# Ten products with C instead of eight on GpSimd in each 24 tiles of a selective scan

## The chip, the core and the metric

The kernel runs on one core of one Trainium2 chip. A core has five engines that run side by side, each with its own queue of instructions: PE (TensorE, matrix products), DVE (VectorE), ACT (ScalarE), POOL (GpSimd) and SP (SyncE, which here issues the transfers). They meet at semaphores. The metric is the time of one execution on the device in microseconds (us); lower is better.

## What is computed

The input is x, 4 images of 96 channels by 64 x 64 pixels, in float32. Four layers follow one another, for each image by itself:

- Layer 0 is a state-space block: layer norm, a projection to 192 inner channels, a 3 x 3 depthwise convolution, and a selective scan over the 4096 pixels in four directions (rows, columns, and both backwards); then a norm, a gate, a projection and an MLP with GELU.
- Layer 1 is a smaller block of the same kind with one state per channel and two directions.
- Layer 2 mixes the tokens by a Fourier transform, followed by an MLP in 8-bit floats.
- Layer 3 is attention without softmax, and again an 8-bit MLP.

The scan of layer 0 is the largest part. For each image, direction, channel d (192) and state n (16) it computes, along the pixels t,

```
h[t] = h[t-1] * exp(dt[t] * A[d,n]) + dt[t] * x[t] * B[n,t]
y[t] = sum over n of h[t] * C[n,t]
```

## The kernel before

**Tiles.** The scan is cut into chunks of 1024 pixels: 4 batches x 4 directions x 4 chunks = 64 chunks. In one chunk there are 192 x 16 = 3072 sequences, which make 24 tiles of 128 partitions (32 channels by 4 states) by 1024 pixels; 1536 tiles in all. The function scan walks them in order. For each tile:

- L745, GpSimd: w = u * B, three tiles ahead (AHEAD). The tiles w lie in a ring of nine (W).
- L144 by way of decay (L731), ScalarE: h = exp(dt * A), two tiles ahead, into a ring of two.
- L821, VectorE: the scan itself, one instruction. It writes its result over w or over h.
- The product with C, in one of two places. If pool_out is true, the scan writes over w, and GpSimd multiplies w by C in place (L841) and copies the last state (L834). If not, the scan writes over h, VectorE multiplies (L829) and ScalarE copies the last state (L837). The copy is left out in the last chunk of a direction.
- L767, PE: the sums over the states, by a matmul with a 0/1 matrix, for pairs of tiles and three tiles later; L779 and L782, VectorE: the sums are added to y.

Which tiles go to GpSimd is decided by a number per batch:

```
POOL_OUT = (5, 8, 8, 8)
...
            pool_out = (x * POOL_OUT[b]) % 24 < POOL_OUT[b]
            o = w if pool_out else h
```

Here x is the tile's place in its chunk, 0 to 23. So 5 of 24 products are on GpSimd in batch 0, spread evenly, and 8 in the other batches.

**What runs beside the scan.** All other work of the program is written as generators, in one queue called stream: the fronts of the four batches (norm, convolution, preparation of dt, u, B and C), then for each batch, once its last direction has begun, its rest: tail (L856, the remainder of layer 0, four tasks of 1024 pixels), l1 (layer 1), transform, middle and back (layers 2 and 3; back ends with four tasks called second). A step of the stream issues some instructions on the engines. Between the instructions of one tile the kernel takes a step if its own account of times lets it:

```
    def advance(free, slack):
        late = max(chain["pe"] - 0.5, now["act"], now["pool"] - 6.0, now["pe"] - 2.0) - free
        if not put_off and late <= slack:
            step()
```

The account (now, chain, t_out and others) is kept while the program is built: each instruction adds its booked time to its engine, for instance 2.36 us for a product on GpSimd and 1.23 us for one on VectorE. So the order of all instructions on each engine is fixed when the program is built, and follows from the booked times. VectorE's part of the steps is put off (later) and issued between the scan's instructions (flush).

While the scan runs, a step works on one task at a time. MLP conversions and additions are given to GpSimd then (aside, L103). When the scan is over, the group in progress is finished (drained), the constants of layer 2 are loaded (L1567, 8 MB), and whatever is left of the stream runs with Now.width = 4: up to four tasks at a time, in tail two, and aside chooses VectorE.

Of the kernel before, what the change touches and what calls it, by code (L numbers as in the profile page):

```python
# [26 lines left out]

DIRS = (0, 1, 3, 2)

POOL_OUT = (5, 8, 8, 8)  # L30

AHEAD, W = 3, 9

# [23 lines left out]
def tile_hybrid(ctx: ExitStack, tc: tile.TileContext, I: dict, out: bass.AP):  # L57
# [597 lines left out]
    def scan(pls, advance, need, last_pass):  # L655
# [146 lines left out]
        for i, (ci, p, g, a) in enumerate(tiles):  # L802
# [12 lines left out]
            h, w = hs.pop(i), ws[i]  # L815
            pool_out = (x * POOL_OUT[b]) % 24 < POOL_OUT[b]
            o = w if pool_out else h
# [890 lines left out]
```

## Time and profile before

| what | us |
|---|---|
| median of 3 runs (6810.67 to 6836.49) | 6822.95 |
| the profiled execution | 6833.64 |
| its span, first to last instruction | 6831.9 |
| first scan starts | 97.2 |
| last scan starts | 6227.9 |
| from the end of the scan to the end of the span | about 600 |

The profile gives for each engine the time in which it was busy. Groups of instructions are shown as line, engine, operation, output<-inputs, shape and count, then the busy time and the mean duration in ns, then the idle time of the engine just before these instructions and the instruction that ended most of it. In the rows by stretch, the first number is the length, and then for each engine stand the busy time and, in brackets, the number of instructions; the granted clock is the share of full speed at which PE ran. A row of waits names the waiting instruction and the one that it waited for. Matmuls in float32 appear as two records each.

### The profile page before, as it was taken

Reading aid. Unit: us, or ns where it says so; the run is one execution under the profiler, and the core shown is the slowest. Engines: PE = TensorE matmul, PEld = TensorE weight load, DVE = VectorE, ACT = ScalarE, POOL = GpSimd, SP = SyncE. Lnnn points to the kernel's source line nnn. Section 1 sums busy time; section 2 is a strip of 40 time slices with the busy share of each in tenths; the row PEclk is TensorE's granted clock in tenths of the full one; section 3 lists DMA queues with packets and bytes.
Section 4 is the critical chain, followed back from the end, with each engine's and each line's share of the span. In section 5 each row is a group of like instructions: output and inputs, shape, how many; then the busy total and the mean of one; then the engine's idle time right before and its main releaser. Section 6 shows DMA issues by size and latency. Waiting matters only on the chain. (4 is left out here: it accounts for less than half of the span.)

```text
span 6831.9 us, 52664 instructions
## 1 busy us (share of the span) xinstructions
PE 4673.5 (68%) x15538; PEld 1514.0 (22%) x15538; DVE 5603.1 (82%) x3872; ACT 3731.0 (55%) x5242; POOL 5188.9 (76%) x2732
## 2 busy tenths in 40 slices
PE   6758667676677666666776675657676666576877
PEld 2112111121112124211111142211111332111353
DVE  3888779797789998998899998898999989984413
ACT  3556546666555545665555455566555456553337
POOL 4888879899779788998688898897887889972000
PEclk8768677686778778766777786668777876676987
DMA  5766666767544348444443375454434563442141
GB/s 149 217 194 193 185 180 192 208 207 210 156 132 143 116 136 262 137 146 144 134 151 125 98 262 155 131 158 139 143 128 127 189 209 127 133 144 83 43 125 37
DMA packets 502464, 1050.00 MB, mean 154 GB/s; under 512 B 138448, under 2 KB 252178, under 8 KB 501144
## 3 DMA queue, kind: packets, MB, share of 16 engines
q1 hardware_dynamic: 502176, 1046.63, 49.5%
q8 instruction: 123, 2.02, 0.1%
q14 instruction: 165, 1.35, 0.1%
HBM read 831.15 MB, written 211.09 MB: 153 GB/s over the span
## 5 line engine op out<-in xcount | busy, mean ns | idle before, releaser
L745 POOL TENSOR_TENSOR w<-u,bb 128x1024 f32<-128x1024 f32 x1536 | 3587.5, 2358 | 179.5 <-PE py L767 123.8
L144 ACT ACTIVATE h<-dt,negA 128x1024 f32<-128x1024 f32 x1536 | 1706.8, 1117 | 795.6 <-DVE w L829 429.2
L821 DVE TENSOR_TENSOR_SCAN h<-h,state,w 128x1024 f32<-128x1024 f32 x804 | 1886.8, 2347 | 271.9 <-ACT h L144 202.8
L829 DVE TENSOR_TENSOR w<-h,cc 128x1024 f32<-128x1024 f32 x1072 | 1309.0, 1221 | 56.7 <-DMA cc<-bc_d 18.8
L767 PE MATMUL py<-w,idup 128*32 128x512 f32 x6144 | 1125.3, 805 | 244.1 <-POOL w L841 80.9
L841 POOL TENSOR_TENSOR w<-w,cc 128x1024 f32<-128x1024 f32 x464 | 1092.0, 2353 | 188.3 <-DVE w L821 142.4
L821 DVE TENSOR_TENSOR_SCAN w<-h,state,w 128x1024 f32<-128x1024 f32 x348 | 814.5, 2341 | 50.9 <-ACT h L144 29.2
L837 ACT COPY state<-h 128x1 f32<-128x1 f32 x804 | 127.5, 159 | 1279.4 <-DVE w L829 1278.6
L821 DVE TENSOR_TENSOR_SCAN h<-h,w 128x1024 f32<-128x1024 f32 x268 | 612.9, 2287 | 103.6 <-ACT h L144 73.5
L98 PE MATMUL pc<-xp 97*64 97x512 f32 (+1 forms) x1152 | 400.2, 611 | 12.4 <-DMA xp<-wc_d 7.8
L767 PEld LDWEIGHTS py<-w,idup 128*32 128x32 f32 x6144 | 164.5, 126 | 1057.3 <-issue 597.3
L834 POOL COPY state<-w 128x1 f32<-128x1 f32 x348 | 64.3, 185 | 363.9 <-DVE w L821 363.1
L111 POOL TENSOR_TENSOR u<-dt,xi 128x512 f32<-128x512 f32 x160 | 216.8, 1371 | 156.7 <-ACT dt L144 142.3
L821 DVE TENSOR_TENSOR_SCAN w<-h,w 128x1024 f32<-128x1024 f32 x116 | 264.4, 2279 | 71.9 <-POOL w L745 55.1
L98 PE MATMUL pc<-xp,wc 96*96 96x512 f32 x576 | 275.1, 631 | 25.6 <-ACT u L144 25.6
L98 PE MATMUL pd<-xd,dtw 6*64 6x512 f32 (+1 forms) x512 | 211.4, 983 | 92.8 <-ACT xd L148 59.1
L98 PE MATMUL pcen<-t,cen 96*96 96x512 f32 x192 | 137.5, 853 | 161.3 <-POOL t L1332 78.8
L144 ACT ACT_TABLE_LOAD x176 | 225.8, 1283 | 32.0 <-PE pd L98 18.1
L136 ACT ACT_TABLE_LOAD x174 | 223.2, 1283 | 3.8 <-PEq L1698 0.7
L98 PEld LDWEIGHTS pc<-xp 97*64 97x64 f32 (+1 forms) x1152 | 149.9, 167 | 270.2 <-issue 239.4
L98 PE MATMUL po<-hq,q 128*96 128x512 fp8e5 x192 | 88.7, 586 | 163.0 <-POOL hq L1320 132.1
L98 PE MATMUL pvar<-sq,avg 96*96 96x512 f32 x256 | 168.9, 801 | 45.3 <-ACT sq L144 45.3
(242 smaller groups left out, 6330.8 us busy)
## 6 DMA issues: line engine op xcount, KB each, us to landing
u<-u_d SPq DMA_DIRECT2D x384, 512.0 KB
dt<-dt_d SPq DMA_DIRECT2D x384, 512.0 KB
bb<-bc_d SPq DMA_DIRECT2D x256, 512.0 KB
cc<-bc_d SPq DMA_DIRECT2D x256, 512.0 KB
dt_d<-dt SPq DMA_DIRECT2D x128, 256.0 KB
u_d<-u SPq DMA_DIRECT2D x128, 256.0 KB
f_d<-fo SPq DMA_DIRECT2D x64, 384.0 KB
a<-f_d SPq DMA_DIRECT2D x64, 384.0 KB
```

The source lines that it names most:

```text
L98: nc.tensor.matmul(o, lhsT=lhsT, rhs=rhs, **kw)
L111: aside(0.2 + size(o) * 2.1e-3, o, a, b).tensor_mul(o, a, b)
L136: nc.scalar.preload_act_table_set("natural_log_exp_and_others")
L144: nc.scalar.activation(o, i, func, **kw)
L745: pool.tensor_mul(w, us[ci, 2 * p + a], bbs[ci, g])
L767: nc.tensor.matmul(o, lhsT=idup, rhs=v, **flags)
L821: dve.tensor_tensor_scan(o[:, r], h[:, r], w[:, r], state if step else 0.0, ALU.mult, ALU.add)
L829: dve.tensor_mul(w, o, cc)
L834: pool.tensor_copy(state, o[:, last : last + 1])
L837: nc.scalar.copy(state, o[:, last : last + 1])
L841: pool.tensor_mul(w, o, cc)
```

## The change

From batch 1 on, 10 of 24 products with C are done by GpSimd instead of 8. Batch 0 keeps its 5.

```
-POOL_OUT = (5, 8, 8, 8)
+POOL_OUT = (5, 10, 10, 10)
```

The tiles that go to GpSimd are chosen by the same formula, so their places in a chunk change as well: with 8 it is each third tile, with 10 each second or third. For these tiles the scan writes over w instead of over h, GpSimd does the product and the copy of the state, and VectorE and ScalarE do neither. The booked times follow, and with them the places at which steps of the stream stand between the tiles.

## The prediction

> **What bounds the kernel now.** I read three views in this order: the page (which engines are loaded), the busy times by stretch (one row per batch of the scan, then what follows the scan), and the waits of VectorE and GpSimd inside the three batches that the change touches. From the page:
>
> ```profile
> PE 4673.5 (68%) x15538; PEld 1514.0 (22%) x15538; DVE 5603.1 (82%) x3872; ACT 3731.0 (55%) x5242; POOL 5188.9 (76%) x2732
> ...
> L745 POOL TENSOR_TENSOR w<-u,bb 128x1024 f32<-128x1024 f32 x1536 | 3587.5, 2358 | 179.5 <-PE py L767 123.8
> L821 DVE TENSOR_TENSOR_SCAN h<-h,state,w 128x1024 f32<-128x1024 f32 x804 | 1886.8, 2347 | 271.9 <-ACT h L144 202.8
> L829 DVE TENSOR_TENSOR w<-h,cc 128x1024 f32<-128x1024 f32 x1072 | 1309.0, 1221 | 56.7 <-DMA cc<-bc_d 18.8
> L841 POOL TENSOR_TENSOR w<-w,cc 128x1024 f32<-128x1024 f32 x464 | 1092.0, 2353 | 188.3 <-DVE w L821 142.4
> ```
>
> The product with C costs 1.22 us on VectorE and 2.35 us on GpSimd. Both engines are heavily loaded, so which one is late has to be read by stage. Busy time by stretch (columns: length, then PE, weight loads, VectorE, ScalarE, GpSimd, granted clock, DMA); the first four rows are batches 0 to 3 of the scan, the fifth is the tail of the last batch that was left over, the sixth the rest of the program:
>
> ```profile
> 97.00:1641.00 1544.00, 1105.32 (x3438) 297.23 (x3439) 1301.14 (x787) 895.51 (x1197) 1325.45 (x713) 0.73 0.66 198
> 1641.00:3158.00 1517.00, 996.67 (x3399) 316.51 (x3397) 1369.41 (x930) 839.07 (x1173) 1294.82 (x675) 0.73 0.49 155
> 3158.00:4707.00 1549.00, 1047.23 (x3487) 332.36 (x3488) 1383.24 (x954) 854.14 (x1201) 1284.77 (x664) 0.74 0.48 152
> 4707.00:6233.00 1526.00, 1024.58 (x3482) 328.82 (x3480) 1380.71 (x951) 852.62 (x1195) 1266.71 (x656) 0.74 0.45 143
> 6233.00:6320.00 87.00, 53.60 (x72) 14.24 (x72) 11.38 (x17) 20.05 (x30) 0.00 (x0) 0.59 0.33 122
> 6320.00:6832.00 512.00, 402.49 (x1544) 209.61 (x1544) 153.28 (x225) 245.64 (x413) 1.55 (x8) 0.83 0.26 68
> ```
>
> Batches 1 to 3 take 4592 us, in which VectorE is busy 4133 and GpSimd 3846: VectorE has the larger load and is idle 459 us. GpSimd is only 287 us below it. After the scan GpSimd does nothing, and the end is set by PE, ScalarE and transfers. Who is waited for in batches 1 to 3 (total us, times, longest):
>
> ```profile
> DVE h L821 <- ACT h L144: 207.4, 114, 13.5
> DVE y L779 <- PE py L767: 44.9, 21, 6.7
> DVE y L782 <- PE py L767: 44.4, 13, 10.3
> DVE h L821 <- POOL w L745: 29.5, 21, 3.0
> ...
> POOL state L834 <- DVE w L821: 343.9, 139, 11.9
> POOL w L841 <- DVE w L821: 132.8, 52, 8.6
> POOL w L745 <- PE py L767: 116.2, 52, 6.3
> ```
>
> VectorE waits for ScalarE's decay and PE's sums, hardly for GpSimd; GpSimd waits 477 us for the scans. Four single stretches show the extremes: one where VectorE binds, one where GpSimd binds, and the two clocks of the leftover tail.
>
> ```profile
> 2243.00:2553.00 310.00, 205.94 (x677) 61.92 (x680) 294.67 (x237) 153.76 (x210) 249.81 (x123) 0.74 0.39 123
> 2816.00:3158.00 342.00, 198.20 (x677) 55.60 (x676) 323.22 (x210) 220.86 (x323) 330.29 (x179) 0.70 0.42 136
> 6259.00:6304.00 45.00, 40.39 (x44) 9.39 (x45) 6.68 (x9) 10.13 (x16) 0.00 (x0) 0.50 0.07 18
> 6304.00:6320.00 16.00, 13.21 (x29) 4.85 (x27) 4.28 (x7) 9.91 (x14) 0.00 (x0) 0.96 0.00 0
> ```
>
> **The change: what moves.** Two tiles of each 24 change sides, in 48 chunks: 96 products. VectorE loses 96 x 1.221 = 117 us. GpSimd gains 96 x 2.353 = 226 us, and 72 state copies (the last chunk of a direction has none) at 0.185 = 13 us, together 239. ScalarE loses those 72 copies at 0.159 = 11 us; it is 55% busy, so I count nothing.
>
> The rest of a batch is placed by the planner, which books 2.36 us for every GpSimd product. In its account a chunk is 24 x 2.35 + 16 x 1.23 + 3 x 0.7 = 78.2 us of VectorE against 24 x 2.36 + 8 x 2.55 = 77.0 of GpSimd before, and 75.7 against 82.1 now. So by its books GpSimd is late, and it lets fewer steps of the rest run beside each scan. The built order of the changed kernel shows it: of the last batch's four tail tasks all four now stand behind the last scan (one before: 8 pca<-ya matmuls instead of 2), and of batch 2's last stage two whole tasks and a third MLP (12 pt matmuls instead of 8, 66 po<-hq instead of 48). That is 156 matmuls more, 61 VectorE and 144 ScalarE instructions more after the scan; the number of transfers is the same. Counted at the mean durations of their rows, 44 us of VectorE and 16 us of GpSimd work leave the scan with them.
>
> **The scan, batches 1 to 3.** VectorE 4133 - 117 - 44 = 3972, GpSimd 3846 + 239 - 16 = 4069. GpSimd becomes the larger load, but the larger load falls from 4133 to 4069: -64 us. What is idle on top of it is the unknown. Before it is 459. The nearest row with both engines evenly loaded is batch 0: 1544 - 1325 = 219 idle, three times that is 657, which makes 4726 (+134). The other end: VectorE's waits for ScalarE and PE (207, 45 and 44, with the smaller ones for state and in-place scans 361) vanish under GpSimd's time wherever GpSimd is the larger. Summing the built order's work by chunk, that is 28 of 48 chunks: 211 us less. I keep 459, since the waits come from steps of the rest, whose number hardly changes, less about 20 for the three tail tasks that leave (the last 223 us of the scan, 6010 to 6233, hold 40 of idle): 4508, -84 us. A product on GpSimd also frees its ring buffer later, so the 116 us that inputs wait for PE's sums may grow by a quarter, 29; and it frees h at the end of the scan and not 1.2 us after it, which helps the decay. I let these two cancel; both lie within the ends.
>
> A rule that speaks against the change: the Trainium skill, GPSIMD Engine Reference, section Performance versus the Vector engine, has two-input elementwise work on GpSimd 1.96 times as long and says to leave it to VectorE. The rows here say 2.353 / 1.221 = 1.93. Taken as a verdict it would cost 96 x 1.13 = 109 us in the scan; the rows say that the two run side by side and the sum goes by the larger load.
>
> **Behind the scan.** Before, the leftover tail takes 87 us, 6233 to 6320: 26 until its x lands behind the 8 MB of constants that are issued at that moment, then 61 for one task of 73 matmul records. Now four things stand there.
> - The MLP in progress: three times two copies and a relu (2 x 0.58 + 1.15), a cast, six po, two copies, 1.15 and the addition: about 17 us.
> - Two tasks of layer 3, alone: the same plus pt, centring, variance and rsqrt, about 11 more at half clock: 28 each, 56. They cover the constants' transfer.
> - The tail's loads, which stand on SP's queue behind the last store: 5 us.
> - Two groups of two tail tasks, 144 records each. At clock 0.50 a record took 45 / 44 = 1.0 us, at 0.96 it took 0.45 us of PE time. At full clock a group is 144 x 0.45 = 65, at half clock 150; at the 0.83 of what follows a record is 0.45 x 0.96 / 0.83 = 0.52, 144 of them 75, and with some 15 of dependent steps I take 90: 180.
>
> Together 17 + 56 + 5 + 180 = 258, against 87: +171 us (121 with full clock, 291 with half clock). The other 512 us stay as they are, in the same order.
>
> The Trainium skill, TensorE: Matmul & The Clock Gate, Part 1, has the half clock end after about 3.4 us of sustained matmuls. By it this group would take 65 us and the term +121. The row contradicts it: 0.50 for 45 us with PE busy 40.
>
> **Sum.** -84 + 171 = +87 us. The profiled execution took 6833.6 (span 6831.9), 11 above the median of 6823; on the median the change makes 6910. About 0.5% (34 us) is what a measurement of this kernel can tell from no change.
>
> **The rivals.**
> - Faster: GpSimd's load hides VectorE's waits. For it: in 2816 to 3158 GpSimd is busy 330 of 342. Against it: the waits cluster in the tails, where VectorE stays as loaded as GpSimd. Price: up to 211, so -295 + 171 = -124, 6699. It decides from 87 us hidden, a quarter of the 361; at 121 the gain can be measured. Chance 0.14.
> - No change: half as much, about 90 hidden, 6820. Chance 0.11.
> - Even load costs as in batch 0: scan +134, with the epilogue +305, 7128. For it: two engines in lockstep lose each other's waits. Against it: batch 0's fronts have more table loads and prepare steps. Chance 0.10.
> - The end runs at half clock: 291 in place of 171, 7030. For it: the leftover tail's first 45 us. Chance 0.12.
>
> **How the numbers follow.** My case has 0.53, with its own range 6860 to 6985 (40 either way in the scan, 45 in the tails). The 80% range reaches down to part of the hidden waits and up to the half clock: 6800 to 7030. Slower by over 0.5% is my case and the last two, 0.75; within 0.5% 0.11; faster 0.14.
>
> **What would show it.** Right: products on GpSimd 560, on VectorE 976; in batches 1 to 3 GpSimd busy near 4070 and above VectorE; the last scan near 6145 on the profile's time, and about 770 us behind it instead of 600. VectorE's wait for GpSimd's inputs rises from 31 to above 100 us. Wrong: the scan ends before 6050 (waits hidden) or after 6250 (waits grown), or the four tail tasks take under 115 us or over 250.

## The result and the profile after

Eight runs of the changed kernel have a median of 6891.5 us (6850.6 to 6902.1), eight of the kernel before 6833.0 (6810.7 to 6851.7; the three named ahead of the prediction are among them). The ratio is 1.0088, 95% interval 1.0068 to 1.0108: 0.9% slower. The profiled execution took 6892.0 us with a span of 6890.2, against 6833.6 and 6831.9 before: +58.

From the page of the changed kernel, the load of each engine and the products with B (L745) and with C (L841 on GpSimd, L829 on VectorE):

```profile
PE 4704.5 (68%) x15538; PEld 1528.7 (22%) x15538; DVE 5505.4 (80%) x3784; ACT 3712.1 (54%) x5155; POOL 5406.7 (78%) x2892
...
L745 POOL TENSOR_TENSOR w<-u,bb 128x1024 f32<-128x1024 f32 x1536 | 3590.1, 2359 | 157.4 <-PE py L767 106.0
...
L841 POOL TENSOR_TENSOR w<-w,cc 128x1024 f32<-128x1024 f32 x560 | 1317.2, 2352 | 148.0 <-DVE w L821 98.5
...
L829 DVE TENSOR_TENSOR w<-h,cc 128x1024 f32<-128x1024 f32 x976 | 1191.7, 1221 | 52.4 <-DMA cc<-bc_d 17.9
```

The 96 products have moved, and each costs what it cost before. The busy times by stretch show where the time went. The first four rows are batches 0 to 3 of the scan, the fifth is what was left over of tails and layer 3, the sixth the rest (length; PE, weight loads, VectorE, ScalarE, GpSimd; clock; DMA).

```profile
97.00:1645.00 1548.00, 1107.80 (x3439) 299.68 (x3440) 1303.36 (x788) 895.46 (x1197) 1325.94 (x713) 0.73 0.67 197
1645.00:3130.00 1485.00, 976.65 (x3345) 312.82 (x3344) 1324.97 (x889) 809.32 (x1105) 1356.90 (x720) 0.73 0.50 158
3130.00:4623.00 1493.00, 968.17 (x3358) 311.62 (x3358) 1330.17 (x896) 809.62 (x1111) 1349.96 (x716) 0.73 0.47 150
4623.00:6127.00 1504.00, 997.39 (x3372) 319.11 (x3370) 1332.43 (x898) 818.62 (x1126) 1351.42 (x716) 0.72 0.47 147
6127.00:6378.00 251.00, 206.53 (x366) 60.01 (x364) 57.69 (x80) 108.86 (x170) 5.23 (x4) 0.73 0.25 75
6378.00:6890.00 512.00, 404.40 (x1544) 210.23 (x1544) 152.91 (x224) 246.11 (x413) 1.56 (x8) 0.83 0.26 67
```

Batches 1 to 3 take 4482 us instead of 4592: the scan is 110 us shorter. What was left over takes 251 us instead of 87, and the final stretch 512 as before. With 4 us more in batch 0 that is the +58. GpSimd now has the larger load in each of the three batches. The waits there have shifted with it (waiting line, total us, times, longest):

```profile
DVE h L821 <- ACT h L144: 146.0, 86, 11.0
DVE y L782 <- PE py L767: 72.5, 18, 10.2
DVE h L821 <- POOL w L745: 71.6, 66, 3.3
...
POOL state L834 <- DVE w L821: 147.9, 79, 6.5
POOL w L745 <- PE py L767: 100.1, 32, 12.4
POOL w L841 <- DVE w L821: 76.4, 29, 7.0
```

VectorE waits for GpSimd's inputs for 72 us instead of 30 (85 instead of 31 with the in-place scans), and GpSimd waits 224 us for the scans instead of 477.

The left-over stretch in its parts: the MLP in progress, two tasks of layer 3, the first pair of tail tasks with its loads, the second pair.

```profile
6127.00:6145.00 18.00, 12.13 (x36) 3.40 (x35) 3.46 (x5) 10.54 (x15) 5.23 (x4) 0.70 0.10 23
6145.00:6195.00 50.00, 22.56 (x43) 7.27 (x42) 10.74 (x14) 27.78 (x41) 0.00 (x0) 0.63 0.54 205
6195.00:6306.00 111.00, 105.53 (x146) 28.90 (x147) 20.59 (x29) 35.42 (x57) 0.00 (x0) 0.61 0.25 61
6306.00:6378.00 72.00, 66.31 (x144) 20.44 (x142) 22.91 (x33) 35.12 (x57) 0.00 (x0) 0.99 0.07 19
```

The two pairs do the same work, 144 matmul records each (the first pair's row counts two of a neighbour). At a clock of 0.61 a pair takes 111 us with PE busy 105.5, at 0.99 it takes 72 with PE busy 66.3.

### The profile page after: what moved, and what is told of

It is laid out like the page before. It is cut to its first block, busy times and chain, and to the rows that moved or that the text cites. A ratio compares the mean times of both kernels' runs of the same rounds, so it can differ in the third digit from the quotient of the medians.

```text
span 6890.2 us, 52656 instructions
## 1 busy us (share of the span) xinstructions
PE 4704.5 (68%) x15538; PEld 1528.7 (22%) x15538; DVE 5505.4 (80%) x3784; ACT 3712.1 (54%) x5155; POOL 5406.7 (78%) x2892
## 5 line engine op out<-in xcount | busy, mean ns | idle before, releaser
L745 POOL TENSOR_TENSOR w<-u,bb 128x1024 f32<-128x1024 f32 x1536 | 3590.1, 2359 | 157.4 <-PE py L767 106.0
L821 DVE TENSOR_TENSOR_SCAN h<-h,state,w 128x1024 f32<-128x1024 f32 x732 | 1717.6, 2346 | 253.1 <-ACT h L144 178.5
L841 POOL TENSOR_TENSOR w<-w,cc 128x1024 f32<-128x1024 f32 x560 | 1317.2, 2352 | 148.0 <-DVE w L821 98.5
L767 PE MATMUL py<-w,idup 128*32 128x512 f32 x6144 | 1148.2, 815 | 384.9 <-POOL w L841 146.8
L829 DVE TENSOR_TENSOR w<-h,cc 128x1024 f32<-128x1024 f32 x976 | 1191.7, 1221 | 52.4 <-DMA cc<-bc_d 17.9
L821 DVE TENSOR_TENSOR_SCAN w<-h,state,w 128x1024 f32<-128x1024 f32 x420 | 983.5, 2342 | 90.9 <-ACT h L144 42.7
L821 DVE TENSOR_TENSOR_SCAN h<-h,w 128x1024 f32<-128x1024 f32 x244 | 557.7, 2286 | 86.4 <-POOL w L745 48.5
L821 DVE TENSOR_TENSOR_SCAN w<-h,w 128x1024 f32<-128x1024 f32 x140 | 319.3, 2281 | 93.4 <-ACT h L144 66.5
L98 PE MATMUL px<-xi,xw 128*96 128x512 f32 (+1 forms) x192 | 140.6, 999 | 89.0 <-ACT xi L144 83.9
```

The costliest lines, as they stand in the source:

```text
L98: nc.tensor.matmul(o, lhsT=lhsT, rhs=rhs, **kw)
L745: pool.tensor_mul(w, us[ci, 2 * p + a], bbs[ci, g])
L767: nc.tensor.matmul(o, lhsT=idup, rhs=v, **flags)
L821: dve.tensor_tensor_scan(o[:, r], h[:, r], w[:, r], state if step else 0.0, ALU.mult, ALU.add)
L829: dve.tensor_mul(w, o, cc)
L841: pool.tensor_mul(w, o, cc)
```

## The experiments

Two things change at once: which engine multiplies, and where the steps of the rest stand. They can be parted, because the second comes only from the booked times. In all experiments but the last the account has its own number, BOOK, beside POOL_OUT. The edit, with the numbers of the first:

```
-POOL_OUT = (5, 8, 8, 8)
+POOL_OUT = (5, 10, 10, 10)
+BOOK = (5, 8, 8, 8)
...
+            booked = (x * BOOK[b]) % 24 < BOOK[b]
...
-            advance(now["dve"] + (0.0 if pool_out else 1.2), FIRST)
+            advance(now["dve"] + (0.0 if booked else 1.2), FIRST)
...
             if not pool_out:
                 dve.tensor_mul(w, o, cc)
+            if not booked:
                 t_out[i] = tick("dve", 1.23)
...
             if pool_out:
                 pool.tensor_mul(w, o, cc)
+            if booked:
                 t_out[i] = tick("pool", 2.36, t_out[i])
```

The booked time of the state's copy follows BOOK in the same way.

**Ten products, booked as eight.** The products move, the steps stay.

> Ten products of 24 on GpSimd, but the account books them as eight, so every step of the rest stands where it stood before. Theory (the loss of the change is the work that moved behind the scan; the products themselves shorten it): behind the scan 599 us as before; in batches 1 to 3 VectorE 4133 - 117 = 4016 busy, GpSimd 3846 + 239 = 4085, and on the larger 424 to 459 idle: 4509 to 4544 against 4592, ratio to before 0.988 to 0.993. Rival (the scan became shorter only because 60 us of the rest left it): the scan stays at 4592 or grows, ratio 1.000 to 1.008.

Measured: ratio 0.9982 (0.9967 to 0.9997). Batches 1 to 3, the left-over tail and the final stretch:

```profile
1642.00:6231.00 4589.00, 3071.05 (x10367) 987.15 (x10365) 4022.73 (x2737) 2541.58 (x3495) 4075.42 (x2162) 0.74 0.47 150
6231.00:6318.00 87.00, 53.62 (x72) 14.24 (x72) 11.24 (x17) 20.05 (x30) 0.00 (x0) 0.61 0.33 121
6318.00:6829.60 511.60, 402.23 (x1544) 209.49 (x1544) 153.07 (x225) 245.75 (x413) 1.55 (x8) 0.83 0.26 68
```

The steps did stay: with the products and state copies left out, the traces show the same order of instructions on PE, VectorE, ScalarE and GpSimd as before (and the next experiment's trace the same order as the changed kernel's). Behind the scan everything is as before. VectorE has lost 111 us of work and GpSimd gained 229, near the 117 and 239 reckoned, but the scan is only 3 us shorter in the trace, and the timed median 11. The theory wanted 48 to 83. The rival is nearer, though its lowest ratio, 1.000, lies just above the interval.

**Eight products, booked as ten.** POOL_OUT as before, and

```
+BOOK = (5, 10, 10, 10)
```

> The other half alone: eight products of 24 on GpSimd, booked as ten, so the steps of the rest stand as in the changed kernel. Theory: behind the scan 764 us (+165); VectorE 3988 + 117 = 4105, GpSimd 4058 - 239 = 3819, scan 4105 + 424 to 459 = 4529 to 4564 (-28 to -63); ratio to before 1.015 to 1.020. Rival (the steps alone made the scan shorter): scan 4482, ratio 1.008, the same as the changed kernel.

Measured: ratio 1.0107 (1.0084 to 1.0131). Batches 1 to 3, and all that follows:

```profile
1642.00:6133.00 4491.00, 2968.44 (x10086) 949.43 (x10088) 4092.82 (x2778) 2449.57 (x3415) 3830.27 (x1982) 0.72 0.47 151
6133.00:6896.00 763.00, 611.23 (x1904) 269.78 (x1896) 210.30 (x304) 353.83 (x582) 6.80 (x12) 0.79 0.25 70
```

The steps alone make the scan 101 us shorter, with VectorE at 4093 us, 41 less than before, and what follows 164 longer. The rival's 4482 is 9 us off; of the ratios, the theory's 1.015 lies well above the interval and the rival's 1.008 just below it. The two halves add up: -0.2% and +1.1% make the +0.9% of the change. So the loss is the displaced work, as predicted; but most of the gain in the scan is its leaving as well, and the products give 3 to 9 us by the traces.

**Twelve products, booked as eight.**

```
-POOL_OUT = (5, 8, 8, 8)
+POOL_OUT = (5, 12, 12, 12)
+BOOK = (5, 8, 8, 8)
```

> Twelve of 24 on GpSimd, booked as eight. Theory (the time of the scan goes by the larger load): GpSimd 3846 + 478 = 4324, VectorE 3898; with 300 to 459 idle 4624 to 4783 in batches 1 to 3, ratio to before 1.005 to 1.028, slower than with ten by 1.5% or more. Rival (GpSimd's load hides VectorE's waits): 211 us idle or less, 4535, ratio 0.992.

Measured: ratio 1.0082 (1.0053 to 1.0111). The scan takes 4638 us with GpSimd busy 4308, so 330 are idle on the larger load. Length and ratio are at the low end of the theory. Its third figure missed: twelve is 1.0% slower than ten, not 1.5% or more. Two more products cost 49 us here, the two before them nothing.

**Nine products, booked as eight.**

```
-POOL_OUT = (5, 8, 8, 8)
+POOL_OUT = (5, 9, 9, 9)
+BOOK = (5, 8, 8, 8)
```

> Nine of 24 on GpSimd, booked as eight. Theory: VectorE 4133 - 59 = 4074, GpSimd 3846 + 120 = 3966; the larger load is 4074, within 15 us of that with ten, and the time is too: ratio to before 0.986 to 0.993. Rival (ten and more hide waits): ten is faster than nine by more than 0.5%.

Measured: ratio 0.9957 (0.9936 to 0.9978), scan 4573 us. The gain is smaller than the theory's 0.7% to 1.4%, and ten is not faster than nine: the rival falls.

**What the totals hide.** I cut the traces at the first scan of each chunk, took in each of the 48 chunks of batches 1 to 3 the larger of VectorE's and GpSimd's busy time, and summed:

| kernel | length of batches 1 to 3 | sum of the larger by chunk | over it | length, last direction (three batches) |
|---|---|---|---|---|
| before | 4592 | 4195 | 397 | 342, 381, 398 |
| nine, booked eight | 4573 | 4207 | 366 | 348, 400, 403 |
| ten, booked eight | 4589 | 4223 | 366 | 359, 407, 400 |
| twelve, booked eight | 4638 | 4345 | 293 | 376, 400, 398 |
| eight, booked ten | 4491 | 4136 | 355 | 344, 349, 350 |
| changed (ten, booked ten) | 4482 | 4172 | 310 | 348, 353, 355 |

By chunk, the larger load does not fall when two more products move everywhere; it rises by 28 us. Summed by direction, a coarser stage, it falls by 4 (4142 to 4138), where the larger of the two totals falls by 58. The last direction is the one where GpSimd has least to spare: layers 2 and 3 give it 34 to 37 us of conversions and additions there (5 to 28 us of steps in the other directions). In batch 1 it already has the larger load, in batch 2 the two are even; in batch 3 VectorE has it (344 against 312). The last direction of batches 1 and 2, before:

```profile
2816.00:3158.00 342.00, 198.20 (x677) 55.60 (x676) 323.22 (x210) 220.86 (x323) 330.29 (x179) 0.70 0.42 136
4326.00:4707.00 381.00, 239.99 (x715) 64.59 (x715) 335.96 (x225) 226.75 (x326) 335.33 (x177) 0.70 0.47 145
```

and with ten, booked as eight:

```profile
2807.00:3165.00 358.00, 203.81 (x676) 57.51 (x676) 314.41 (x200) 220.17 (x316) 349.52 (x193) 0.67 0.41 130
4309.00:4716.00 407.00, 259.65 (x711) 69.73 (x711) 327.52 (x216) 224.50 (x316) 352.31 (x191) 0.66 0.44 135
```

GpSimd's 330 become 350 in the first, and the stretch grows from 342 to 358. In the second it goes from 335 to 352, and the stretch from 381 to 407. In batch 3 ten make the two loads even (336 and 335), and the stretch grows by 2. This is the new theory: the larger load of each stage decides, and what one direction gains the last gives back. Two experiments turn it both ways. Both edit the line that picks the tiles, with BOOK = (5, 8, 8, 8) as above.

**The share by direction.**

```
-POOL_OUT = (5, 8, 8, 8)
+POOL_OUT = {0: 10, 1: 10, 3: 9, 2: 8}
...
-            pool_out = (x * POOL_OUT[b]) % 24 < POOL_OUT[b]
+            share = POOL_OUT[k] if b else 5
+            pool_out = (x * share) % 24 < share
```

> From batch 1 on the share of GpSimd goes by the direction of the scan, booked as eight throughout: ten in the first two directions, nine in the third, eight in the last, where layers 2 and 3 give GpSimd conversions and additions. Theory (chunk by chunk the larger of the two loads decides, and it lies with VectorE in the first three directions and with GpSimd in the last): from the runs so far, by direction, -22, -9, -17 and 0 us against the kernel before: scan of batches 1 to 3 4544, ratio to before 0.991 to 0.996, at least as fast as nine throughout (0.9957). Rival (these differences are chance): 0.996 to 1.000.

Measured: median 6777.2, ratio 0.9941 (0.9918 to 0.9964). The scan and what follows it:

```profile
1644.00:6169.00 4525.00, 3040.16 (x10366) 987.04 (x10364) 4064.56 (x2773) 2542.56 (x3522) 3989.14 (x2099) 0.74 0.48 152
6169.00:6769.00 600.00, 458.30 (x1616) 224.61 (x1616) 164.24 (x240) 266.32 (x443) 1.55 (x8) 0.80 0.27 76
```

The scan is 67 us shorter in the trace (48 were expected; the timed median is 46 lower) and nothing is displaced. This version is faster than both kernels. Its interval overlaps the one of the version with nine products in all directions, so it is not shown that it beats that one too.

**Ten in the last direction alone.**

```
+POOL_OUT = {0: 8, 1: 8, 3: 8, 2: 10}
```

> Ten products on GpSimd in the last direction alone, eight in the other three, booked as eight throughout. Theory (GpSimd has the larger load in the last direction, so two more products there cost, though the totals of the batch say otherwise): with ten throughout the last direction took 17, 26 and 2 us more in the three batches; so +45 in the scan, ratio to before 1.003 to 1.009, the three other directions within 15 us of before. Rival (the larger load of a whole batch decides, VectorE's before): a little faster, -15, ratio 0.996 to 1.000.

Measured: ratio 1.0062 (1.0041 to 1.0083), inside the theory's range. In the profiled execution the last direction took 359, 402 and 399 us: 17, 21 and 1 more. Its first two rows:

```profile
2807.00:3166.00 359.00, 204.52 (x677) 57.31 (x676) 314.91 (x201) 220.53 (x316) 349.64 (x193) 0.66 0.41 131
4322.00:4724.00 402.00, 253.91 (x712) 66.89 (x711) 325.93 (x216) 224.73 (x317) 352.18 (x191) 0.66 0.44 137
```

The other three directions together were 33 us shorter than before, more than the 15 that I had allowed, and that execution, 6846 us, was the fastest of its eight (median 6866). So a direction in a single trace is good to some 15 us; the verdict rests on the timed ratio.

Together the two runs show where two more products help and where they cost: by the timed medians -46 us with the share by direction, +46 with ten in the last direction alone, and -11 with ten in all. The last direction repeats from trace to trace: 342, 381, 398 and 340, 382, 393 with eight; 359, 407, 400 and 359, 402, 399 with ten. That the larger load of the stage is the reason is shown in part. Against the kernel before, it changes as follows, by direction and by chunk, with the timed median beside it:

| kernel, booked eight | larger load by direction | by chunk | timed median |
|---|---|---|---|
| share by direction | -48 | -22 | -46 |
| nine | -4 | +12 | -33 |
| ten | -4 | +28 | -11 |
| ten in the last direction | +25 | +31 | +46 |
| twelve | +166 | +150 | +53 |

By direction the signs are right, but not all the amounts; by chunk nine and ten have the wrong sign. Each count also puts the products at other places in the chunk; what the places alone do is not tested.

**What a displaced step costs.** Eight products, booked as nine, displaces less:

```
+BOOK = (5, 9, 9, 9)
```

> Eight products of 24 on GpSimd, booked as nine: three tail tasks of the last batch stand behind the scan instead of one, one after another, and none of layer 3's tasks is displaced. Theory (displaced work costs more behind the scan than it saves in it): behind the scan 26 + 3 x 45 to 61 = 161 to 209 in place of 87 (+74 to +122); in the scan 45 to 65% of the 101 us that booking ten saved (-45 to -65); ratio to before 1.002 to 1.011. Rival (the displacement is harmless up to some amount): 0.997 to 1.000.

Measured: ratio 1.0028 (1.0013 to 1.0044). The scan takes 4539 us (-53), and the three tail tasks 146 in place of 87 (+59), less than the 74 to 122 expected:

```profile
1645.00:6184.00 4539.00, 3027.96 (x10200) 961.75 (x10199) 4107.95 (x2798) 2502.03 (x3497) 3844.57 (x1994) 0.73 0.48 151
6184.00:6330.00 146.00, 125.35 (x240) 36.41 (x238) 36.70 (x51) 61.14 (x91) 0.00 (x0) 0.84 0.28 92
```

The trace shows why: the 26 us of waiting for loads did not come (PE waited 0.8 us before the first of the three tasks), and the tasks began 45 us apart, the low end of the 45 to 61 reckoned.

The other extreme puts the rest of all batches behind the scan:

```
+    rests = []
-    scan(pls, advance, need, lambda b: stream.append(rest(b)))
+    scan(pls, advance, need, rests.append)
...
+    for b in rests:
+        stream.append(rest(b))
     while step():
```

The constants of layer 2 that are loaded after the scan serve the first rest only; each later one loads its own (whole.clear() after whole_pool.close()).

> The products as before, but the rest of all four batches stands behind the scan, four tasks at a time; only the fronts run beside it. Theory (a step costs more behind the scan than in it, since beside the scan it fills gaps): batches 1 to 3 take 48 x 77.8 = 3734 us of VectorE's own loop plus 20 to 170 of waits and fronts, 3750 to 3900 in place of 4592; the program behind the scan grows from 599 by 3.6 rests of 590 to 640; together +1300 to +1500, ratio 1.19 to 1.22. So a whole rest costs some 200 us in the scan and 600 behind it. Rival (a displaced step costs as much as it saves): ratio near 1.0, and a rest costs the scan 500 us or more.

Measured: 8171.3 us in one run, 1.20 of before. Batches 1 to 3, and all that follows:

```profile
1646.00:5340.00 3694.00, 1357.30 (x4654) 206.05 (x4652) 3636.15 (x2064) 1397.37 (x1751) 3621.05 (x1838) 0.56 0.43 143
5340.00:8169.00 2829.00, 2306.76 (x7331) 1037.62 (x7328) 786.55 (x1141) 1271.81 (x2112) 6.27 (x32) 0.81 0.26 73
```

The scan is 898 us shorter, the program behind it 2230 longer: displaced, a step costs 2.5 times what it costs beside the scan. The scan's 3694 us lie below the 3750 to 3900 expected. Without steps VectorE is busy 3636 of them; the larger load by chunk sums to 3660, with 35 over it. So some 360 of the 397 us over the larger load before come with the steps. They make the scan wait for ScalarE and PE: VectorE waited 229 us for the decays and 89 for the sums before, and waits 6 us for the decays and never for the sums here.

## Why the prediction came out right, and where its working was wrong

The forecast was +87 us, slower with 0.75; measured are +58, on the medians of the same runs and in the profile alike. All but 4 us in batch 0 lies in the two terms that were named.

- The booking, and through it the order: right, and shown. Booked as eight, ten products cost nothing (0.9982); eight booked as ten cost 1.1%.
- Behind the scan: +171 forecast, +164 measured. The MLP took 18 (17 forecast), the two tasks of layer 3 with their end 50 (56), the tail tasks with their loads 183 (185). The final stretch stayed at 512.
- The Trainium skill, TensorE: Matmul & The Clock Gate, Part 1, would have ended the half clock after about 3.4 us of sustained matmuls. The changed kernel's first pair again shows otherwise: 0.61 over 111 us with PE busy 105.5, and only the second pair ran at 0.99. The forecast took 0.83 and 90 us for each pair; 111 and 72 came. That the sum fits is luck.
- The loads in the scan: VectorE 3972 forecast and 3988 measured, GpSimd 4069 and 4058. What was idle on GpSimd was forecast at 439 and measured at 424. The last scan was forecast near 6145 and began at 6121; VectorE's wait for GpSimd was to rise above 100 us and rose to 85. GpSimd's wait for PE's sums was to grow by a quarter and fell from 116 to 100.
- The step that failed: "the larger load falls from 4133 to 4069: -64 us". It took the larger of two totals. With the products moved and the steps in their old places, the larger total falls from 4133 to 4075, and the scan was 3 us shorter (11 by the timed medians). The larger load has to be summed by stage: by direction it falls by 4, and by chunk it rises by 28.
- The second failure hides the first: "less about 20 for the three tail tasks that leave" was sized by the idle time of one stretch. The steps that left shorten the scan by 101. The forecast had -64 for the products and -20 for the steps; the runs show -3 to -9 and some -101. That the forecast's -84 for the scan comes near the measured -110 is therefore luck.
- The rival that GpSimd's load hides waits: part of it is real. What lies over the larger load by chunk falls from 397 to 366 with ten and to 293 with twelve. Against that the larger load by chunk grows by 28 with ten and by 150 with twelve, so it hardly pays with ten and not at all with twelve; with nine it grows by 12 and what lies over it falls by 31, and there it pays. The rival of an even load that costs as in batch 0 (657 idle on GpSimd) did not come; 424 were idle.

## What to carry to other kernels

Balance two engines stage by stage, not over the whole: here a share that gave GpSimd nine or ten products in the first three directions and eight in the last gained 0.6%, and ten in the last direction alone cost 0.6%. Nine throughout gained 0.4%, which these runs cannot tell from the 0.6%, and ten throughout 0.2%. Where a planner places other work by booked times, a change of one booking moves that work too; keep the booking apart from the edit, and look in the built order at what falls behind the end of the main loop, where no other engine covers it.

## What the runs showed of the hardware

VectorE and GpSimd side by side hardly slowed each other. In the kernel before, the 907 products of VectorE with GpSimd busy for over nine tenths of their time took 1.222 us on average, the 77 with GpSimd busy for under a tenth 1.218; for GpSimd's products it is 2.354 (366) against 2.349 (28). The kernel places h in PSUM, the memory that PE writes, and cc in SBUF, so VectorE's product reads only one of its inputs from SBUF; no run here shows what two would do.

PE's granted clock stayed at 0.50 from 6195 to 6260 us of the changed kernel although PE was busy for 59.5 of those 65 us:

```profile
6195.00:6260.00 65.00, 59.53 (x66) 13.63 (x66) 5.84 (x8) 16.50 (x27) 0.00 (x0) 0.50 0.41 98
```

Equal work took 111 us in one pair of tail tasks and 72 in the next. What ends the half clock is not shown.
